# Padding the products of the scans and of the STU to 128 rows, and keeping half of the scan projections in DRAM

**Chip, cores, metric.** One core of a Trainium2 chip (trn2). Time is device microseconds of one execution; lower is better. All runs compared here are of the fast state. "PE" is TensorE, "PEld" its weight loads, DVE VectorE, ACT ScalarE, POOL GpSimd, SP SyncE, which issues nearly all transfers (DMA).

## The reference, cut to what matters

Input is 4 x 48 x 48 x 128 in float32. Layer 0 is a selective scan over the image in four directions (rows, columns, and both backwards); layer 1 is attention and then the STU, a sum of causal convolutions with 16 spectral filters.

```python
# layer 0, of each image; d = 256, N = 16 states, R = 8, K = 4 directions, L = 2304 positions
xs = stack([x0, x1, x0[..., ::-1], x1[..., ::-1]])       # directions 2 and 3 are 0 and 1 backwards
x_dbl = einsum('bkdl,kcd->bkcl', xs, x_proj_w)           # 8 + 16 + 16 rows a direction
dts_r, Bs, Cs = x_dbl[:, :, :R], x_dbl[:, :, R:R+N], x_dbl[:, :, R+N:]
dt = softplus(einsum('bkrl,kdr->bkdl', dts_r, dt_proj_w) + dt_proj_b)
def step(h, inp):
    h = h * exp(dt * A) + (dt * u) * B                   # 256 channels x 16 states
    return h, sum_n(h * C)
# layer 1: t = t + attention(ln(t)); t = t + stu(ln(t))
# stu: for 16 filters k, u convolved with phi_k (and with alternating signs), then projected and summed
```

## The kernel before

The scans run in 24 chunks of 384 positions for each image, a chunk in 8 units (half of the channels, a quarter of the states), a unit as one step ("slot") of a loop that also prepares later chunks and feeds TensorE with pieces of the STU of the image before. Names in the views: xd holds the projections of a chunk, dt, B and y are the products around the scan (`s`), dA its exp, rep holds dt and dt times x for the scans, bc a row of B or C. Of the STU, tt is a piece of the filters, cv a convolution, Q a copy of one by ScalarE, U the sum of both that VectorE makes, pr the projection with the weights G.

```python
class Chunk:
    def prep(self, pool):            # a generator: two steps of it are taken in each slot
        yield
        xd = self.xd = pool.xd.tile([64, CS], F32, ...)                  # two buffers
        bcd = self.bcd = dram.tile([32, CS], F32, ...)
        ps = mm_tile(...)
        for h in range(NH):
            nc.tensor.matmul(ps[:64, :CS], xw[:, h, k, :], in_order(xc[h], k, self.lo, CS), ...)
        yield 2 * CS
        nc.scalar.activation(xd, ps[:64, :CS], AF.Identity, bias=onerow)  # rows: 8 of dt, a one, 32 of B and C
        yield
        for h in range(NH):
            ps = mm_tile(...)
            nc.tensor.matmul(ps[:, :CS], dtw[:, k, h * P:(h + 1) * P], xd[:R + 1], ...)   # 9 rows
            yield CS
            nc.scalar.copy(re[:, h, 0], ps[:, :CS])
            if h == 0:
                nc.sync.dma_start(bcd, xd[32:64])
            yield
        ...                          # softplus, times x, store to DRAM (dtdud)
        load(0)                      # rep: four transfers of 384 KB each, from dtdud
        yield
        yield 0
        load(1)
        yield
    def fetch(self, i, pool):        # a row of B or C, spread over 32 partitions, from bcd
        ...
class Unit:
    def spread(self, ps):            # rows of B to 128 partitions: 32 rows
        nc.tensor.matmul(self.bt[:, :CS], spread[32:64, self.q]..., self.ch.xd[32:64], ...)
    def sum_c(self, ps):             # y: four products side by side, each into 32 partitions
        for g in range(G4):
            nc.tensor.matmul(ch.y[g * DL:(g + 1) * DL, :CS], csum, self.s[:, g], ...)

def prepare(s):                      # twice a slot; ci chunk, j slot in it; TURN = 4
    for c in [ci + 1] * (j <= TURN + 1) + [ci + 2] * (j >= TURN):
        done[0] += next(preps[c], None) or 0

# STU: conv(n, c, g), blocks of 128 rows of u, the last of 64 rows (KP = [128, 128, 128, 128, 64])
x = (sums[:kp, J, g], u[:kp, J, 2 + g], u[:kp, J, g])[c]
nc.tensor.matmul(p2[:, :, at - first:], x, t[:kp, :, ...], ...)
```

## Time and profile before

| | before |
|---|---|
| time, median of the runs | 7045.9 us |
| scan stage 0 (with the mixing of STU weights) | 1090 us |
| scan stages 1, 2, 3 (with the STU of the image before) | 1308, 1307, 1309 us |
| STU of the last image alone, at the end | 743 us |
| attention and the rest | about 1290 us |

A scan stage is counted from the start of its first scan to the start of its last, to about 1 us. The page gives the engines' shares and then forty slices; a digit is tenths of a slice, 9 is 90% or more, and PEclk is the clock that TensorE was granted.

```profile
PE 5958.7 (85%) x25224; PEld 3407.3 (48%) x25224; DVE 4944.7 (70%) x6193; ACT 2846.0 (40%) x5101; POOL 3877.9 (55%) x1815
...
PE   4666666878899999788899999887899999889999
...
PEclk6667676888999999888999999888999999899999
```

The three humps of 9s in the row of PE are scan stages 1 to 3, the last four slices the STU alone. The clock is at 0.8 or more throughout them.

### The profile page before, as it was taken

What the parts mean: (1) busy time and instruction counts of PE and PEld (TensorE: products, weight loads), DVE (VectorE), ACT (ScalarE), POOL (GpSimd) and SP (SyncE); (2) the same over time, 40 slices, a digit from 0 to 9 for tenths busy, and PEclk for the clock granted to TensorE, in tenths of its full rate; (3) what the DMA queues carried; (4) which work ended last, traced back from release to release, by engine and by line L of the source; (5) the groups of instructions that cost most, each with busy time, mean ns of one, the idle gap of its engine ahead of it and who ended that gap; (6) DMA issues with size and microseconds to landing.
All of it is one profiled execution on the core that took longest, in us unless ns stands there. A gap on an engine that the chain in (4) does not pass through costs nothing.

```text
span 7051.1 us, 75955 instructions
## 1 busy us (share of the span) xinstructions
PE 5958.7 (85%) x25224; PEld 3407.3 (48%) x25224; DVE 4944.7 (70%) x6193; ACT 2846.0 (40%) x5101; POOL 3877.9 (55%) x1815
## 2 busy tenths in 40 slices
PE   4666666878899999788899999887899999889999
PEld 1222222533455556533455556533445556547788
DVE  7889898457888987557888987457888987422111
ACT  3555554334444543234445543233444543231000
POOL 2888888126677876115677876205677876300000
PEclk6667676888999999888999999888999999899999
DMA  4655554046777787135777877126777877215545
GB/s 100 138 138 121 139 126 128 19 97 137 165 185 188 193 202 198 42 82 133 165 191 187 202 192 201 48 70 135 164 179 188 204 190 194 76 47 141 157 143 176
DMA packets 648905, 1018.90 MB, mean 145 GB/s; under 512 B 93849, under 2 KB 506649, under 8 KB 623778
## 3 DMA queue, kind: packets, MB, share of 16 engines
q1 hardware_dynamic: 642816, 1010.84, 57.3%
q10 hardware_dynamic: 5698, 3.21, 0.2%
q8 instruction: 201, 3.29, 0.2%
q14 instruction: 190, 1.56, 0.1%
HBM read 895.86 MB, written 117.84 MB: 144 GB/s over the span
## 4 chain that ended last, share of the span: by engine, by line
PE 48%; DVE 24%; DMA 12%; ACT 6%; POOL 4%; issue 4%; SPq 2%; ACTq 0%; DVEq 0%; POOLq 0%
PE cv L926 22%; DVE s L435 12%; PE pr L984 6%; DMA rep<-dtdud 4%; DVE s L427 4%; PE y L452 4%; PE s L687 3%; PE o L680 3%; DMA bc<-bcd 3%; POOL s L444 3%; PE B L419 3%; DVE re L382 2%; DMA tt<-fd 2%; PE xp L350 2%; PE op L623 2%
## 5 line engine op out<-in xcount | busy, mean ns | idle before, releaser
L444 POOL TENSOR_TENSOR s<-s,bc 128x1536 f32<-128x1536 f32 x768 | 2652.0, 3453 | 298.1 <-DVE s L435 195.2
L435 DVE TENSOR_TENSOR_SCAN s<-dA,carry,s 128x384 f32<-128x384 f32 x2560 | 2429.7, 999 | 358.1 <-ACT dA L432 357.6
L432 ACT ACTIVATE dA<-rep,A 128x384 f32<-128x384 f32 x3072 | 1768.5, 584 | 1436.0 <-DVE s L435 1423.5
L926 PE MATMUL cv<-tt,u 128*128 128x256 f32 (+4 forms) x7680 | 1701.8, 362 | 140.3 <-DVE U L946 133.5
L926 PEld LDWEIGHTS cv<-tt,u 128*128 128x128 f32 (+1 forms) x7680 | 1288.1, 193 | 720.9 <-issue 303.7
L946 DVE TENSOR_TENSOR U<-cv,Q 128x256 f32<-128x256 f32 (+1 forms) x1280 | 487.1, 388 | 912.9 <-PE cv L926 910.8
L427 POOL TENSOR_TENSOR s<-rep,bc 128x1536 f32<-128x1536 f32 x288 | 993.2, 3449 | 95.0 <-DMA bc<-bcd 95.0
L926 PE MATMUL cv<-tt,us 128*128 128x256 f32 (+4 forms) x3840 | 897.6, 371 | 149.0 <-DVE U L946 111.2
L452 PE MATMUL y<-s,csum 128*32 128x384 f32 x6144 | 749.3, 563 | 210.9 <-POOL s L444 122.8
L427 DVE TENSOR_TENSOR s<-rep,B 128x1536 f32<-128x1536 f32 x480 | 834.4, 1738 | 94.5 <-PE B L419 57.9
L926 PEld LDWEIGHTS cv<-tt,us 128*128 128x128 f32 (+1 forms) x3840 | 652.3, 197 | 429.7 <-DVE U L946 160.1
L935 ACT COPY Q<-cv 128x256 f32<-128x256 f32 (+3 forms) x640 | 224.7, 352 | 1473.2 <-PE cv L926 1331.3
L984 PE MATMUL pr<-U,G 128*128 128x512 f32 (+4 forms) x2048 | 753.1, 500 | 68.2 <-DVE U L946 36.5
L443 POOL COPY carry<-s 128x4 f32<-128x4 f32 x640 | 145.9, 228 | 1005.4 <-DVE s L435 872.5
L419 PE MATMUL B<-xd,spread 32*128 32x384 f32 x960 | 494.7, 598 | 73.4 <-DVE s L427 72.7
L984 PEld LDWEIGHTS pr<-U,G 128*128 128x128 f32 x2048 | 350.0, 201 | 296.2 <-issue 168.9
L435 DVE TENSOR_TENSOR_SCAN s<-dA,s 128x384 f32<-128x384 f32 x512 | 455.6, 937 | 50.0 <-ACT dA L432 50.0
L452 PEld LDWEIGHTS y<-s,csum 128*32 128x32 f32 x6144 | 128.1, 114 | 658.1 <-issue 318.7
L687 PE MATMUL s<-xnT 128*128 128x512 f32 (+1 forms) x720 | 358.2, 583 | 50.0 <-ACT e L689 26.7
L799 PE MATMUL G<-M,W 128*128 128x128 f32 (+2 forms) x768 | 232.0, 452 | 162.5 <-DMA M<-in_M_phi_plus 109.5
L156 POOL TENSOR_TENSOR ln_vu<-ln_vu,mhalf 128x4 f32<-128x4 f32 (+1 forms) x20 | 31.4, 1572 | 610.6 <-DVE ln_vu L155 610.6
L689 ACT ACTIVATE e<-s,shift 128x512 f32<-128x512 f32 (+1 forms) x360 | 230.8, 644 | 325.7 <-PE s L687 325.4
(155 smaller groups left out, 3965.8 us busy)
## 6 DMA issues: line engine op xcount, KB each, us to landing
rep<-dtdud SPq DMA_DIRECT2D x768, 384.0 KB, 8.4
tt<-fd SPq DMA_DIRECT2D x192, 577.0 KB, 4.6
bc<-bcd SPq DMA_DIRECT2D x2304, 48.0 KB, 3.6
tt<-fd SPq DMA_DIRECT2D x192, 513.0 KB, 4.6
tt<-fd SPq DMA_DIRECT2D x192, 385.0 KB, 4.2
dtdud<-re SPq DMA_DIRECT2D x768, 96.0 KB, 2.2
G<-gd SPq DMA_DIRECT2D x192, 256.0 KB, 4.7
tt<-fd SPq DMA_DIRECT2D x64, 514.0 KB, 5.6
```

Source lines behind the costliest of these rows:

```text
L419: nc.tensor.matmul(self.bt[:, :CS], spread[32:64, self.q].rearrange("p c j -> p (c j)"), self.ch.xd[32:64], start=True, stop=True)
L427: eng.tensor_tensor(s, self.ch.rep[self.h][:, 1], bt.unsqueeze(1).to_broadcast([P, G4, CS]), ALU.mult)
L432: nc.scalar.activation(dA[:, :CS], ch.rep[self.h][:, 0, g], AF.Exp, scale=A[:, ch.k, self.h * G4 + g, self.q:self.q + 1])
L435: nc.vector.tensor_tensor_scan(s, dA[:, CS - 1::-1] if ch.rev else dA[:, :CS], s, 0.0 if ch.first else carry[:, self.h, self.q, g:g + 1], ...
L444: nc.gpsimd.tensor_tensor(self.s, self.s, ch.bc[Q4 + self.q].unsqueeze(1).to_broadcast([P, G4, CS]), ALU.mult)
L452: nc.tensor.matmul(ch.y[g * DL:(g + 1) * DL, :CS], csum, self.s[:, g], start=(self.q == 0), stop=(self.q == Q4 - 1))
L687: nc.tensor.matmul(p[:, :w], xnT[:, i * P:(i + 1) * P], xnT[:, 512 * J:512 * J + w], start=True, stop=True)
L689: nc.scalar.activation(e[:, :w], p[:, :w], AF.Exp, bias=shift)
L799: nc.tensor.matmul(p[:, :n] if j else p[:, NF - 1 - i], W[:, q if t else 0, i], M[t][:, i].unsqueeze(1).to_broadcast([P, n, C]) if j else ...
L926: nc.tensor.matmul(p2[:, :, at - first:], x, t[:kp, :, hi - 1 - at + J * P:end if end >= 0 else None:-1], start=(J == 0), stop=(J == nb - 1))
L946: nc.vector.tensor_tensor(dst, src, q, ALU.add)
L984: nc.tensor.matmul(p[:, :, :v], Gs[n][:, q, x, :], U[n][:, 4 * q:4 * q + 4, :v], start=False, stop=(k == KF - 1 and q == 1 and v == w))
```

## The change

The intent: every product of the scans and of the STU gets 128 rows (zeros in the weights or in the data where there were fewer), so that TensorE does not change its shape between them. And since directions k and k + 2 project the same positions, one product of 128 columns gives both (64 rows each); it is computed for directions 0 and 1, stored to DRAM, and directions 2 and 3 load it. The diff, cut to its core (the layout of the weights on the host follows from it):

```diff
-            xd = self.xd = pool.xd.tile([64, CS], F32, tag="xd", name=f"xd{name}")
-            bcd = self.bcd = dram.tile([32, CS], F32, tag="bcd", name=f"bcd{name}")
-            ps = mm_tile(f"xp{name}")
-            for h in range(NH):
-                nc.tensor.matmul(ps[:64, :CS], xw[:, h, k, :], in_order(xc[h], k, self.lo, CS), ...)
-            yield 2 * CS
-            nc.scalar.activation(xd, ps[:64, :CS], AF.Identity, bias=onerow)
+            xd = self.xd = pool.xd.tile([P, CS], F32, tag="xd", name=f"xd{name}")
+            xdd_ = xdd[k % 2][self.lo // CS]
+            if k < 2:
+                ps = mm_tile(f"xp{name}")
+                for h in range(NH):
+                    nc.tensor.matmul(ps[:, :CS], xw[:, h, k, :], in_order(xc[h], k, self.lo, CS), ...)
+                yield 2 * CS
+                nc.scalar.activation(xd, ps[:, :CS], AF.Identity, bias=onerow)
+            else:
+                yield 0
+                nc.sync.dma_start(xd, xdd_)
             yield
 ...
-                nc.tensor.matmul(ps[:, :CS], dtw[:, k, h * P:(h + 1) * P], xd[:R + 1], ...)
+                nc.tensor.matmul(ps[:, :CS], dtw[:, k, h * P:(h + 1) * P], xd, ...)
                 yield CS
                 nc.scalar.copy(re[:, h, 0], ps[:, :CS])
-                if h == 0:
-                    nc.sync.dma_start(bcd, xd[32:64])
+                if h == 0 and k < 2:
+                    nc.sync.dma_start(xdd_, xd)
 ... # fetch reads its row from xdd; spread has a variant for each half of xd
-            nc.tensor.matmul(self.bt[:, :CS], spread[32:64, self.q]..., self.ch.xd[32:64], ...)
+            nc.tensor.matmul(self.bt[:, :CS], spread[:, self.ch.k // 2, self.q]..., self.ch.xd, ...)
 ... # STU; the unused half of the last block is set to zero once an image
-                x = (sums[:kp, J, g], u[:kp, J, 2 + g], u[:kp, J, g])[c]
-                nc.tensor.matmul(p2[:, :, at - first:], x, t[:kp, :, ...], ...)
+                x = (sums[:, J, g], u[:, J, 2 + g], u[:, J, g])[c]
+                nc.tensor.matmul(p2[:, :, at - first:], x, t[:, :, ...], ...)
```

More of the change, by code (lines that the diff above doesn't have):

```diff
@@ L79, in hybrid_kernel @@
     cb = load("cb", [P, NH], a["conv_b"].rearrange("(h p) -> p h", p=P))
-    xw = load("xw", [P, NH, K, 64], a["x_proj_wT"].rearrange("(h p) k r -> p h k r", p=P))
-    dtw = load("dtw", [R + 1, K, D], a["dt_proj_wT"])
+    xw = load("xw", [P, NH, 2, P], a["x_proj_wT"].rearrange("(h p) k r -> p h k r", p=P))
+    dtw = load("dtw", [P, K, D], a["dt_proj_wT"])
     A = load("A", [P, K, NH * G4, Q4], a["A_logs"])
@@ L114, in hybrid_kernel @@
     nc.vector.tensor_scalar_mul(nident, ident, -1.0)
-    onerow = wp.tile([64, 1], F32, name="onerow")
+    onerow = wp.tile([P, 1], F32, name="onerow")
     nc.vector.memset(onerow, 0.0)
-    nc.gpsimd.affine_select(onerow, onerow, pattern=[[0, 1]], compare_op=ALU.not_equal, fill=1.0,
-                            base=-R, channel_multiplier=1)
-    spread = wp.tile([64, Q4, C4, DL], F32, name="spread")
+    spread = wp.tile([P, 2, Q4, C4, DL], F32, name="spread")
     nc.vector.memset(spread, 0.0)
-    nc.gpsimd.affine_select(spread, spread, pattern=[[-C4, Q4], [-1, C4], [0, DL]],
-                            compare_op=ALU.not_equal, fill=1.0, base=-32, channel_multiplier=1)
+    for v in range(2):
+        nc.gpsimd.affine_select(onerow, onerow, pattern=[[0, 1]], compare_op=ALU.not_equal, fill=1.0,
+                                base=-R - 64 * v, channel_multiplier=1)
+        nc.gpsimd.affine_select(spread[:, v], spread[:, v], pattern=[[-C4, Q4], [-1, C4], [0, DL]],
+                                compare_op=ALU.not_equal, fill=1.0, base=-32 - 64 * v, channel_multiplier=1)
     csum = wp.tile([P, DL], F32, name="csum")
@@ L138, in hybrid_kernel @@
     fd = res.tile([KF, 3, 2, LF + P], F32, name="fd")
+    xdd = [[res.tile([P, CS], F32, name=f"xdd{k}_{c}") for c in range(L // CS)] for k in range(2)]
     def tokens(x, J):
@@ L345, in prep @@
             yield
-            xd = self.xd = pool.xd.tile([64, CS], F32, tag="xd", name=f"xd{name}")
-            bcd = self.bcd = dram.tile([32, CS], F32, tag="bcd", name=f"bcd{name}")
-            ps = mm_tile(f"xp{name}")
-            for h in range(NH):
-                nc.tensor.matmul(ps[:64, :CS], xw[:, h, k, :], in_order(xc[h], k, self.lo, CS),
-                                 start=(h == 0), stop=(h == NH - 1))
-            yield 2 * CS
-            nc.scalar.activation(xd, ps[:64, :CS], AF.Identity, bias=onerow)
+            xd = self.xd = pool.xd.tile([P, CS], F32, tag="xd", name=f"xd{name}")
[3 more added lines that the diff above has]
+                for h in range(NH):
+                    nc.tensor.matmul(ps[:, :CS], xw[:, h, k, :], in_order(xc[h], k, self.lo, CS),
+                                     start=(h == 0), stop=(h == NH - 1))
+                yield 2 * CS
[3 more added lines that the diff above has]
+                nc.sync.dma_start(xd, xdd_)
             yield
@@ L358, in prep @@
                 ps = mm_tile(f"dt{name}_{h}")
-                nc.tensor.matmul(ps[:, :CS], dtw[:, k, h * P:(h + 1) * P], xd[:R + 1], start=True, stop=True)
+                nc.tensor.matmul(ps[:, :CS], dtw[:, k, h * P:(h + 1) * P], xd, start=True, stop=True)
                 yield CS
                 nc.scalar.copy(re[:, h, 0], ps[:, :CS])
-                if h == 0:
-                    nc.sync.dma_start(bcd, xd[32:64])
+                if h == 0 and k < 2:
+                    nc.sync.dma_start(xdd_, xd)
                 yield
@@ L404, in fetch @@
             t = self.bc[i] = pool.one.tile([P, CS], F32, tag=f"bc{i}", name=f"bc{self.name}_{i}")
+            src = xdd[self.k % 2][self.lo // CS]
             for c in range(C4):
-                nc.sync.dma_start(t[c * DL:(c + 1) * DL], self.bcd[4 * i + c].partition_broadcast(DL))
+                row = 64 * (self.k // 2) + 32 + 4 * i + c
+                nc.sync.dma_start(t[c * DL:(c + 1) * DL], src[row].partition_broadcast(DL))
     class Unit:
@@ L418, in spread @@
             self.bt = ps.tile([P, 512], F32, tag="B", name=f"B{self.name}")
-            nc.tensor.matmul(self.bt[:, :CS], spread[32:64, self.q].rearrange("p c j -> p (c j)"),
-                             self.ch.xd[32:64], start=True, stop=True)
+            nc.tensor.matmul(self.bt[:, :CS], spread[:, self.ch.k // 2, self.q].rearrange("p c j -> p (c j)"),
+                             self.ch.xd, start=True, stop=True)
         def enter(self, pool):
@@ L466, in hybrid_kernel @@
     FETCHED = sorted({q for h, q in POOLED} | set(range(Q4, 2 * Q4)))
-    CHUNK_COLS = (len(quads) - len(POOLED)) * CS + len(quads) * CS + 4 * CS
+    CHUNK_COLS = (len(quads) - len(POOLED)) * CS + len(quads) * CS + 3 * CS
     def begin_scans(b, pool):
@@ L810, in begin_stu @@
                  keep.tile([P, NM, 2, C], F32, tag="us", name=f"us{b}"))
+        for t in us[b]:
+            nc.gpsimd.memset(t[KP[-1]:, NM - 1], 0.0)
     def tail(b, J, T, po, pool, ps):
@@ L922, in conv @@
             for J in range(nb):
-                at, kp = max(first, J * P) if J else first, KP[J]
+                at = max(first, J * P) if J else first
                 end = J * P - 1
-                x = (sums[:kp, J, g], u[:kp, J, 2 + g], u[:kp, J, g])[c]
-                nc.tensor.matmul(p2[:, :, at - first:], x, t[:kp, :, hi - 1 - at + J * P:end if end >= 0 else None:-1],
+                x = (sums[:, J, g], u[:, J, 2 + g], u[:, J, g])[c]
+                nc.tensor.matmul(p2[:, :, at - first:], x, t[:, :, hi - 1 - at + J * P:end if end >= 0 else None:-1],
                                  start=(J == 0), stop=(J == nb - 1))
@@ L1125 @@
     l0, l1 = "L0_conv_", "L1_ffn_"
-    xw = np.zeros((D, K, 64), np.float32)
+    xw = np.zeros((D, 2, P), np.float32)
     xp = i[l0 + "x_proj_w"].transpose(2, 0, 1)
-    xw[:, :, :R] = xp[:, :, :R]
-    xw[:, :, 32:] = xp[:, :, R:]
+    dtw = np.zeros((P, K, D), np.float32)
+    for k in range(K):
+        at = 64 * (k // 2)
+        xw[:, k % 2, at:at + R] = xp[:, k, :R]
+        xw[:, k % 2, at + 32:at + 64] = xp[:, k, R:]
+        dtw[at:at + R, k] = i[l0 + "dt_proj_w"][k].T
+        dtw[at + R, k] = i[l0 + "dt_proj_b"][k]
     phi = np.zeros((KF, 2, 2, LF + P + 1), np.float32)
@@ L1139 @@
         "x_proj_wT": xw,
-        "dt_proj_wT": np.concatenate([i[l0 + "dt_proj_w"].transpose(2, 0, 1), i[l0 + "dt_proj_b"][None]]),
+        "dt_proj_wT": dtw,
         "A_logs": i[l0 + "A_logs"].reshape(K, NH * G4, DL, Q4, C4).transpose(4, 2, 0, 1, 3).reshape(P, K, NH * G4, Q4),
```

## The prediction

> **What bounds the kernel now.** I read the page first (engine shares, forty slices), then the table by stage, then the chain of waits, then timelines of single chunks. The scans mark the stages: a prologue, four scan stages (one per batch; 24 chunks of 384 positions, 8 units of four scans each), attention after each, and at the end the spectral filter (STU) of the last batch alone. Scans 1 to 3 run with the STU of the batch before them on TensorE.
>
> ```profile
> core 0: us, PE busy (x) PEld busy (x) DVE busy (x) ACT busy (x) POOL busy (x), PEclk, DMA share, GB/s
> ...
> 124.00:1214.00 1090.00, 681.05 (x2700) 255.28 (x2700) 968.46 (x980) 608.41 (x1090) 934.07 (x423) 0.68 0.56 131
> ...
> 1521.00:2829.00 1308.00, 1185.29 (x5400) 672.03 (x5400) 1088.75 (x1305) 595.76 (x1063) 934.27 (x422) 0.95 0.73 179
> ...
> 6308.00:7051.00 743.00, 734.35 (x3460) 581.45 (x3460) 129.72 (x325) 59.13 (x165) 0.00 (x0) 0.99 0.52 153
> ```
>
> So three regimes. Scan stage 0 is bound by VectorE (89% busy, PE 62%). Scan stages 1 to 3 are bound by PE and VectorE together (91% and 83%); cut at the stage, the chain lies about 47% on PE, 23% on VectorE and 16% on DMA. The end is PE alone (99%). PE time is worth all of itself at the end, about half in stages 1 to 3, almost nothing in stage 0.
>
> The end shows what the change is after:
>
> ```profile
> 6852.47 10.38 PE cv L926 x48
> ...
> 6899.88 8.83 PE cv L926 x60
> 6909.77 8.83 PE cv L926 x60
> ```
>
> Each row is one filter k. The first belongs to columns 384 to 512: 256-column products, 10.38 / 48 = 0.216 us each, the streaming rate. The others belong to the last block, 512 to 576: 128-column products should take half, but 8.83 / 60 = 0.147. Instruction by instruction, 128-row products start 0.112 us apart; a 64-row pair (every fifth block of rows) starts 0.204 after the one before it, its second half 0.215 after its first, the next 128-row product 0.200 after that and its second half again 0.215. Extra: 0.092 + 0.103 + 0.088 + 0.103 = **0.386 us per convolution**. Check: 60 x 0.112 + 4 projections x 0.216 + 6 x 0.386 = 9.89, the period of the rows.
>
> In the scan stages the small products show the same:
>
> ```profile
> 2604.97 0.91 PE L926 MATMUL cv<-tt,u 128*128 128x128 f32 x5
> 2605.81 0.91 PE L419 MATMUL B<-xd,spread 32*128 32x384 f32 x2
> 2606.65 0.85 PE L452 MATMUL y<-s,csum 128*32 128x384 f32 x8
> 2607.43 0.82 PE L926 MATMUL cv<-tt,u 128*128 128x130 f32 x5
> ```
>
> A product is two instructions of 384 x 2 cycles, 0.32 us each. B holds PE 0.84 us (2605.81 to 2606.65) where 0.64 is streaming, and its start comes 0.095 late. The y products (four 32-column strips side by side) are a mode of their own.
>
> **What the Trainium skill says.** "TensorEngine Tiling (Array Packing)", Key Properties: "Changing tiling mode (not just tile) drains the TensorE". The trace agrees: 0.09 to 0.10 us at each change of shape between 128*128 and 64*128, 32*128, 128*64 or 128*32. "TensorE: Matmul & The Clock Gate", LDWEIGHTS: a load's time depends on columns, not rows. The trace agrees, so padding with zeros costs no weight-load time, and the 0.32 us a product streams depends on its columns:
>
> ```profile
> L419 PEld LDWEIGHTS B<-xd,spread 32*128 32x128 f32 x960 | 157.2, 204 | 268.7 <-issue 120.8 <-DVE s L427 110.3 <-DVE s L435 18.9
> ...
> L926 PEld LDWEIGHTS cv<-tt,u 64*128 64x128 f32 x512 | 76.5, 187 | 37.5 <-issue 8.8
> ```
>
> (128-row loads take 193.) "DMA: Bandwidth & Descriptors", Queues, rings and completion order: on each DMA engine descriptors are consumed in ring order. The trace agrees: a small store issued behind big loads on the same queue lands behind them (below).
>
> **The change part by part**, for one of scan stages 1 to 3.
> - Last STU block, 64 rows to 128: 16 filters x 6 convolutions x 0.386 = 37 us of PE, all in the last 4 or so chunks (that block has 17.6% of the STU's columns). The same 37 us at the end of the program.
> - B, 32 to 128 rows: loses the entry (0.095) and the second weight load that nothing hides (0.105); the exit into y's mode stays. 0.20 x 118 = 24 us.
> - dt, 9 to 128 rows, between 128-row products: loses entry, inner reload and exit, 0.29 x 44 = 13 us.
> - x_proj: 1.44 us for an even direction and 2.70 for an odd (strided reading), from start of xp to start of what follows it; mean 2.07, plus 0.095 for entry. Half of them go: 12 x 2.17 = 26 us. The others lose entry and exit, 12 x 0.19 = 2 us.
> - Sum: 102 us of PE per stage, of 1308.
> - Added: for directions 2 and 3, a load of xd (192 KB) from DRAM in place of product and copy. 12 per stage, 2.4 MB against some 234 MB (179 GB/s x 1308 us): bandwidth is no matter. Latency is.
>
> **The new wait.** In program order the load of xd stands directly behind the second rep load of the chunk before, four transfers of 384 KB, and dt follows half a slot later (a slot is a unit's 6.4 us). Chunk 12 of stage 1:
>
> ```profile
> 2138.59 6.76 SPq L376 DMA_DIRECT2D rep<-dtdud  x4
> ...
> 2145.92 0.41 SPq L363 DMA_DIRECT2D bcd<-xd  x1
> ```
>
> ```profile
> 2142.48 0.91 PE L359 MATMUL dt<-xd,dtw 9*128 9x384 f32 x2
> ```
>
> The last rep transfer lands at 2152.4 and the 48 KB bcd store, issued behind it, at 2153.3. A load of xd would land about there, while dt ran at 2142.5. Over chunks 12 to 23 of stages 1 to 3 the rep load lands 6.5 us after the present start of dt (stage means 6.5, 6.7, 6.6), so xd would land some 7.5 us after it. PE works in order: it stands there. ScalarE stands too, at its copy of dt (today 1 us after dt), so exps stop and soon scans. Against it, what ScalarE waits now for x_proj (52.6 us in 21 waits, 2.5 each) goes for half the chunks, and VectorE has a slack of 1 to 2 us. I take 5 to 6.5 us of bubble per such chunk.
>
> Per stage 1 to 3:
> - 12 chunks of directions 0 and 1: PE saves 5 x 0.20 + 2 x 0.29 + 0.19 = 1.8 us each, half of it in time: -11.
> - 8 chunks of directions 2 and 3 before the last block (now 49.3 us each, PE 47.5, VectorE 44): PE saves 1.0 + 0.6 + 2.2 = 3.8, after which VectorE is the floor at about 45 (stage 0 does a chunk in 45.4 with 40.5 of VectorE; this stage's best is 44.9 with 42.8). With the bubble 50 to 51.5: +1 each, +8.
> - 4 chunks under the last block (now 56): PE saves 3.8 + 37 / 4.2 = 12.6; with the bubble 51: -5 each, -20.
> Together -23, times three -69. The end: -37. Stage 0: products hardly count (-10), but where rep loads are late (every third chunk lands 8 us after the copy of dt) the bubble shows, 4 x 6 to 8 us: +15 to +20 net. Setup (a larger dt weight, two memsets): under 3 us. Sum -69 - 37 + 15 = -91, about **6950 us** (-1.4%).
>
> **Rivals.**
> 1. The load is hidden: SyncE runs ahead of PE, or another wait already covers it. Then the 102 us per stage count half to two thirds: 3 x 50 to 65 + 37 = 190 to 230, and stage 0 gains 10: 6810 to 6850. For it: SyncE is often the one waiting (for PE and VectorE). Against it: the rep transfers take 8.4 us from issue to landing, whoever waits.
> 2. The bubble counts in full on top of what VectorE needs, 8 us for 36 chunks, more in stage 0: 36 x 2.5 + 20 more than my sum, near 7060. For it: all engines stop at once, nothing fills the gap.
> 3. VectorE takes over at once and PE time is worth nothing in the scans: only the 37 us of the end are left, less the bubbles: 7010 or above. Against it: chunks under the last block have PE 95% and VectorE 79% busy.
>
> **Range and chances.** The 37 us at the end are nearly certain. The rest is a difference of two effects of the same size, both about 50 to 80 us per stage; a bubble 1.5 us shorter than mine moves the total by 60 us and over the 2% line (6905). Hence 6950, range 6850 to 7060; faster 0.25, within 2% 0.72, slower 0.03.
>
> **What would show each step right or wrong.** Right: the end stage at 706 us, with 60 products in about 6.7 us; no shapes 9*128, 32*128, 64*128 left in scans and STU, B to y 0.74 us; xp x192. PE waits for the DMA xd<-xdd some 36 to 48 times, 5 to 8 us each, in the view of waits, and ScalarE's wait for dt grows by as much; chunks of directions 2 and 3 are no shorter than those of 0 and 1 late in the stage. Wrong: waits for xdd under 2 us (rival 1), an end stage that stays at 740 (then drains are not from the shape), or stages 1 to 3 over 1310 us (rival 2).

## The result, and the profile after

The changed kernel is correct and takes 7256.9 us (median of 4, 7254.6 to 7261.3): a ratio of 1.029 (95% interval 1.028 to 1.031), slower by 2.9%, where 6950 was predicted with a range of 6850 to 7060. A ratio here is the mean time of one kernel's fast runs over that of the other's of the same rounds, so not quite the ratio of the medians.

| us | before | after | difference |
|---|---|---|---|
| scan stage 0 | 1090 | 1126 | +36 |
| scan stage 1 | 1308 | 1380 | +72 |
| scan stage 2 | 1307 | 1371 | +64 |
| scan stage 3 | 1309 | 1384 | +75 |
| STU at the end | 743 | 707 | -36 |

The attention between them changed by under 2 us each time; the five rows give the difference. First what went as intended. In the chain of waits of the kernel after, the last block at the end stands so:

```profile
7110.31 10.38 PE cv L937 x48
...
7142.57 6.70 PE cv L937 x60
```

60 products in 6.70 us, not 8.83: 0.112 each, as the drains' removal should give, while the 256-column block before it keeps its 10.38. The shapes 9*128, 32*128 and 64*128 are gone from the scans and the STU, and TensorE's busy time fell from 5959 to 5642 us. Yet the kernel is slower. The table by stage, with stage 1 cut in three (the chunks before any load of xd is made, the stretch of twelve chunks in which all twelve are made, the rest), before, then after:

```profile
1521.00:2108.00 587.00, 510.37 (x2021) 263.06 (x2022) 470.88 (x570) 257.37 (x462) 388.17 (x181) 0.91 0.69 161
2108.00:2719.00 611.00, 572.97 (x2743) 337.59 (x2741) 531.38 (x626) 298.97 (x525) 473.07 (x214) 0.98 0.78 198
2719.00:2829.00 110.00, 101.95 (x638) 71.38 (x638) 86.49 (x111) 39.42 (x79) 73.03 (x29) 0.95 0.59 166
```

```profile
1557.00:2125.00 568.00, 479.54 (x2006) 268.49 (x2008) 459.37 (x568) 255.39 (x460) 389.13 (x181) 0.92 0.71 168
2125.00:2833.00 708.00, 558.10 (x2723) 361.52 (x2722) 530.64 (x627) 293.88 (x515) 470.73 (x213) 0.89 0.68 174
2833.00:2938.00 105.00, 86.47 (x628) 65.87 (x628) 84.48 (x111) 39.65 (x78) 73.81 (x30) 0.93 0.61 172
```

Columns: from and to, length, then busy time of PE, PEld, DVE, ACT and POOL, granted clock, DMA share, GB/s. The first part gains 19 us, the last 5; the middle loses 97. There all engines do the same work as before (DVE 531 us in both) in more time, and the clock falls from 0.98 to 0.89. The view of waits of the kernel after (who waited for whom: us in total, times, longest) and of the load's line say why:

```profile
ACT re L368 <- PE dt L366: 480.1, 127, 14.0
...
PE dt L366 <- DMA xd<-xdd: 359.6, 42, 12.5
```

```profile
DMA to landing us min/median/max: 7.3/8.5/11.5
```

TensorE stops 42 times at dt, 8.6 us on average, for a transfer that takes 8.5 us (median) from issue to landing. ScalarE's wait for dt was 166.4 us before. One stop in the timeline (start, length, engine, what, and in brackets what the engine waited for):

```profile
2388.05 2.00 PE L937 MATMUL cv<-tt,u 128*128 128x258 f32 x8 [0.46 <-DVE U L957]
...
2398.72 1.65 PE L366 MATMUL dt<-xd,dtw 128*128 128x384 f32 x2 [8.67 <-DMA tt<-fd]
...
2400.16 3.62 PE L937 MATMUL cv<-tt,us 128*128 128x256 f32 x8
...
2400.41 0.48 ACT L368 COPY re<-dt 128x384 f32<-128x384 f32 x1 [9.63 <-PE dt L366]
2403.82 0.37 ACT L946 COPY Q<-cv 128x256 f32<-128x256 f32 x1 [2.94 <-PE cv L937]
2404.09 1.09 ACT L441 ACTIVATE dA<-rep,A 128x384 f32<-128x384 f32 x2
...
2404.72 1.93 DVE L444 TENSOR_TENSOR_SCAN s<-dA,carry,s 128x384 f32<-128x384 f32 x2 [11.90 <-ACT dA L441]
```

The load was issued at 2389.89 behind four rep transfers (2386.52 to 2389.47). PE stands 8.67 us (the weight load of the same product names xd<-xdd). ScalarE, in order, stands at its copy of dt, then at a copy that needs a convolution behind dt, and only then comes the exp; VectorE stands 11.90. This way through ScalarE is not the usual one: read from the trace, VectorE's longest wait around the stop ends in 24 of the 36 stops of stages 1 to 3 at U, which needs a convolution that stands behind dt on TensorE itself, and in 12 at a scan that needs ScalarE's exp. And the 8 convolution instructions after the stop take 3.62 us where 8 of the same size took 2.00 before it: they run at half clock. The Trainium skill, "TensorE: Matmul & The Clock Gate", Part 1, says that after an idle window of some 3.4 us the clock falls to a half. The trace agrees: TensorE is idle from 2390.06, the clock record stands at 0.5 from 2394.10 to 2404.34, and 1.0 and 0.5 are its only values.

### The profile page after: what moved, and what is told of

It reads as the page before. It is cut to its first block, busy times and chain, and to the rows that moved or that the text cites. A ratio compares the mean times of both kernels' runs of the same rounds, so it can differ in the third digit from the quotient of the medians.

```text
span 7259.6 us, 75560 instructions
## 1 busy us (share of the span) xinstructions
PE 5641.7 (78%) x25032; PEld 3440.7 (47%) x25032; DVE 4893.1 (67%) x6193; ACT 2822.0 (39%) x5053; POOL 3881.9 (53%) x1825
## 4 chain that ended last, share of the span: by engine, by line
PE 40%; DVE 26%; DMA 19%; ACT 5%; issue 4%; SPq 3%; POOL 2%; DVEq 0%; ACTq 0%; POOLq 0%
PE cv L937 18%; DVE s L444 14%; DMA xd<-xdd 5%; PE pr L995 5%; DVE s L436 4%; DMA tt<-fd 4%; DMA bc<-xdd 4%; PE s L696 3%; DMA rep<-dtdud 3%; PE y L461 3%; PE o L689 3%; DVE re L389 2%; PE op L632 2%; PE B L428 2%; DVE xc L264 2%
## 5 line engine op out<-in xcount | busy, mean ns | idle before, releaser
L937 PE MATMUL cv<-tt,u 128*128 128x256 f32 (+3 forms) x7680 | 1680.3, 366 | 285.1 <-DVE U L957 279.6
L937 PEld LDWEIGHTS cv<-tt,u 128*128 128x128 f32 x7680 | 1305.9, 199 | 827.3 <-DVE U L957 360.7
L937 PE MATMUL cv<-tt,us 128*128 128x256 f32 (+3 forms) x3840 | 841.3, 362 | 111.3 <-DVE U L957 61.5
L461 PE MATMUL y<-s,csum 128*32 128x384 f32 x6144 | 730.6, 551 | 199.2 <-POOL s L453 122.3
L937 PEld LDWEIGHTS cv<-tt,us 128*128 128x128 f32 x3840 | 645.7, 198 | 309.1 <-DVE U L957 107.4
L995 PE MATMUL pr<-U,G 128*128 128x512 f32 (+4 forms) x2048 | 731.6, 491 | 65.5 <-DMA G<-gd 43.5
L428 PE MATMUL B<-xd,spread 128*128 128x384 f32 x960 | 444.9, 548 | 111.2 <-DVE s L436 110.9
L366 PE MATMUL dt<-xd,dtw 128*128 128x384 f32 x384 | 212.6, 643 | 398.1 <-DMA xd<-xdd 359.6
```

The source lines that it names most:

```text
L428: nc.tensor.matmul(self.bt[:, :CS], spread[:, self.ch.k // 2, self.q].rearrange("p c j -> p (c j)"), self.ch.xd, start=True, stop=True)
L937: nc.tensor.matmul(p2[:, :, at - first:], x, t[:, :, hi - 1 - at + J * P:end if end >= 0 else None:-1], start=(J == 0), stop=(J == nb - 1))
L995: nc.tensor.matmul(p[:, :, :v], Gs[n][:, q, x, :], U[n][:, 4 * q:4 * q + 4, :v], start=False, stop=(k == KF - 1 and q == 1 and v == w))
```

## The experiments

Theory A: the wait for xd, caused by the load's place behind rep, is the whole loss, and padding gains. Rivals: B, padding or the new spread of the work slows the scans; C, the traffic of the load costs wherever it stands.

| run | edit | us, median | ratio to before (95%) | stages 0 / 1 / 2 / 3 | end |
|---|---|---|---|---|---|
| after | the change | 7256.9 | 1.029 (1.028-1.031) | 1126 / 1380 / 1371 / 1384 | 707 |
| e1_early | load 5 slots earlier | 6869.2 | 0.973 (0.971-0.975) | 1072 / 1265 / 1261 / 1271 | 707 |
| e2_nold | no load: products for all directions | 6887.1 | 0.975 (0.973-0.977) | 1082 / 1265 / 1259 / 1270 | 707 |
| e3_ldonly | before plus the load (wrong result) | 7481.8 | 1.061 (1.057-1.064) | 1129 / 1438 / 1438 / 1438 | 743 |
| e6_warm | after, 8 idle products at the stop | 7248.8 | 1.026 (1.024-1.029) | 1147 / 1364 / 1373 / 1374 | 707 |
| e8_warm13 | after, 13 idle products | 7243.4 | 1.028 (1.025-1.030) | 1157 / 1364 / 1354 / 1361 | 707 |
| e7_early64 | e1_early, last block 64 rows again | 6927.6 | 0.982 (0.980-0.985) | 1072 / 1274 / 1267 / 1279 | 743 |
| e5_first | after, load ahead of rep | 6921.7 | 0.982 (0.980-0.984) | 1078 / 1282 / 1281 / 1278 | 707 |
| e4_actq | after, load on ScalarE's queue | 6961.8 | 0.988 (0.986-0.990) | 1092 / 1289 / 1291 / 1288 | 707 |
| e9_copylater | after, ScalarE's copy a slot later | 7420.9 | 1.053 (1.050-1.055) | 1156 / 1421 / 1420 / 1423 | 707 |
| e10_early_copylater | e1_early, copy a slot later | 6993.3 | 0.992 (0.990-0.995) | 1093 / 1306 / 1296 / 1304 | 707 |

Before took 7063.2, 7052.1 and 7052.7 us (medians) on the chips of the three groups of runs (e1, e2, e3, e6; e7, e8, e5, e4; e9, e10), so medians of different groups compare to some 17 us only. All but e3_ldonly are correct.

**The load, earlier.**

```diff
+        def load_xd(self, pool):
+            self.xd = pool.xd.tile([P, CS], F32, tag="xd", name=f"xd{self.name}")
+            nc.sync.dma_start(self.xd, xdd[self.k % 2][self.lo // CS])
 ... # in prepare, first call of a slot
+            if first_half and j == 0 and ci + 2 < len(chunks) and chunks[ci + 2].k >= 2:
+                chunks[ci + 2].load_xd(front)
 ... # in prep, directions 2 and 3: no load; pool xd=(2, SB) -> xd=(3, SB)
```

> The changed kernel, but the load of xd for directions 2 and 3 is issued about five slots (some 30 us) earlier, at slot 0 of the chunk two before, ahead of both rep loads, into a third xd buffer; same bytes, same products. Theory A (the wait: the load stands behind 1.5 MB of rep in the same queue, and TensorE, ScalarE and VectorE stop for it, 7 us of VectorE 12 times in stage 0 and 9.5 to 10.4 us 36 times in stages 1 to 3): the stops vanish and the gain of padding and of the dropped products is left: 6800 to 6880 us, waits for xd<-xdd under 20 us in all. Rival B (the padded products or the new spread of filter work over the slots slow the scans): stays above 7100. Rival C (the extra DRAM traffic itself, wherever it stands): above 7200.

Measured 6869 us, as theory A has it; the fastest of all. The load's line, and stage 1 in the same three parts as above:

```profile
DMA to landing us min/median/max: 2.3/2.6/4.7
```

```profile
1503.00:2071.00 568.00, 483.32 (x2006) 270.90 (x2010) 458.75 (x568) 255.74 (x460) 389.59 (x181) 0.91 0.71 168
2071.00:2661.00 590.00, 525.03 (x2722) 343.51 (x2714) 530.93 (x627) 294.86 (x515) 470.56 (x213) 0.96 0.82 209
2661.00:2768.00 107.00, 87.33 (x628) 66.95 (x628) 84.83 (x111) 39.99 (x78) 74.43 (x30) 0.92 0.61 169
```

With the same bytes and products, only the middle differs from the changed kernel by more than 2 us, 590 us against 708. Rivals B and C fall. (This run has a third xd buffer too; e5_first below has two and most of the gain.) Twelve stops in a stage cost 1380 - 1265 = 115, 109 and 113 us: **9.4 us each**; in stage 0, 54 us, 4.5 each.

**Padding alone.**

```diff
-            if k < 2:
+            if True:
-                    nc.tensor.matmul(ps[:, :CS], xw[:, h, k, :], ...
+                    nc.tensor.matmul(ps[:, :CS], xw[:, h, k % 2, :], ...
```

> Padding alone: all products with 128 rows, but x_proj is computed for all four directions as before (96 products, each 128 columns wide), no load of xd. Theory A: before minus 37 us at the end minus some 40 per stage of scans 1 to 3 (75 us of TensorE less in each, half of it in time): 6850 to 6930. Rival B (padding slows the scans): 7050 or more.

Measured 6887 us, as expected. It is 18 us (of medians) from e1_early. So half of the x_proj products, some 26 us of TensorE a stage, is worth next to nothing: stages 1 to 3 are the same to 3 us, stage 0 differs by 11. That is a sum: in chunks 12 to 19 the early load is 9 us a stage shorter than this run, under the last block (chunks 20 to 23) 8 longer (mean of stages 1 to 3, read from the traces). The load had little to win.

**The load alone.**

```diff
+            if k < 2:
                 ... # as before
+            else:
+                yield 0
+                nc.sync.dma_start(xd, xdd_)          # 64 rows; 9, 32 and 64-row products stay
```

> The load alone, in the kernel before: products unpadded as before, but directions 2 and 3 load xd (64 rows) from DRAM at the place where the change loads it, in place of x_proj. The result is wrong on purpose (they get the projections of directions 0 and 1). Theory A: the changed kernel plus what padding gains, 7350 to 7450. Rival B: 7040 to 7100, the load costs little and padding is what slows.

Measured 7482 us, 32 above the expected range: the stops cost at least as much in the kernel before (+130 us in each of stages 1 to 3, +39 in stage 0).

**Is it the clock?** The same product, of weights without meaning, over and over into the PSUM tile that dt then overwrites.

```diff
                 ps = mm_tile(f"dt{name}_{h}")
+                if h == 0 and k >= 2:
+                    for i in range(8):               # 13 in e8_warm13
+                        nc.tensor.matmul(ps[:, :CS], win[:, :P], win[:, :CS], start=True, stop=True)
```

> The changed kernel with 8 products of no use (384 columns, two instructions each, 5.1 us at full clock) ahead of the first dt of each chunk of directions 2 and 3, where TensorE stands for 8.4 us anyway. It tests whether a part of the loss is the clock: in the changed kernel the second half of stage 1 has 22 spells at half clock, with 93 us of products in them, against 5 and 22 before. If the half clock after each stop costs about 35 us per stage: 7140 to 7200 us, and the spells fall back to under 10. If the stop alone is the cost: 7250 to 7310, unchanged or a little slower.

> As the run with 8 products of no use, but 13 (8.4 us, the mean length of the stop), because after 8 there were still stops of about 4 us and the products after them still ran at half clock. If half clock after the stop is worth some 35 us a stage: 7130 to 7200 and the second half of stage 1 has under 30 us of products at half clock (93 in the changed kernel, 62 with 8). If the stop alone is the cost: 7240 to 7300 although the half clock is gone.

8 products left stops of about 4 us behind them, and the products after those still ran at half clock (17 spells, not under 10); the total, 7249, is 1 us under the range for the stop alone: no test. 13 close the gap. Second half of stage 1, by the table: the changed kernel, then e8_warm13.

```profile
2244.00:2938.00 694.00, 552.29 (x2940) 369.60 (x2940) 524.58 (x631) 284.63 (x507) 467.52 (x212) 0.90 0.67 176
```

```profile
2250.00:2950.00 700.00, 634.65 (x3283) 416.87 (x3285) 537.53 (x646) 294.40 (x520) 476.65 (x214) 0.96 0.69 179
```

The clock is back at 0.96 (0.98 in the kernel before), products at half clock (matmuls laid over the clock records) fall from 93 to 47 us, though not under the 30 that I had set; e1_early, which has no stops, stands at 44. Half of the 46 us is 23, about what the stages gain: stages 1 to 3 gain 17, 17 and 23 us; stage 0, where the idle products outlast the stop, loses 31, and the total, 7243, lies in the range that I gave for the stop alone. So half clock is a part, about 1.6 us of the 9.4 per stop (19 / 12), and the stop itself is the rest. As the 13 products outlast the shorter stops, 1.6 is rather too low.

**Where does the gain under the last block go?** In e1_early, stages 1 to 3 gain 43, 46 and 38 us over before; my sum had -87 ahead of its bubbles (a chunk at VectorE's floor of 45 plus a bubble of 5.3 makes the 50.3 behind its "+1 each"; twelve such bubbles are 64, and -23 less 64 is -87).

```diff
-                at = max(first, J * P) if J else first
+                at, kp = max(first, J * P) if J else first, KP[J]
 ... # and [:kp] again on both operands
```

> The version with the early load, with the padding of the filter's last block undone (64-row products there again, 96 per batch). It asks where the 37 us of TensorE go that the padding saves in the last quarter of each scan stage 1 to 3. At the end of the program it costs 37 us in any case. Theory A1 (under the last block the scan stages are bound by transfers: with the early load the chunks 20 and 21 take 58 and 61 us, no less than the 57 and 57 of the kernel before, TensorE waits 21 us for tt there and the DMA moves 213 GB/s): the scan stages stay within 8 us each and the total is the early load's plus 37 to 60, 6905 to 6930. Rival A2 (TensorE bounds there, something else made those chunks long): plus 37 and 20 or more in each of three stages, 6965 or above.

Measured: the end +36 us, but stages 1 to 3 only +9, +6 and +8, though 37 us of TensorE by my sum come back in each (its busy time in stage 1 rises by 30, from 1095.7 to 1125.5): A1, at the edge of its limit (total 6928). By the table, the first three chunks under the last block before (2605 to 2779) and with the early load (2541 to 2725):

```profile
2605.00:2779.00 174.00, 164.59 (x992) 111.73 (x990) 135.65 (x170) 69.95 (x132) 116.61 (x58) 0.97 0.80 220
```

```profile
2541.00:2725.00 184.00, 147.62 (x999) 112.38 (x1000) 135.79 (x171) 70.89 (x132) 118.23 (x58) 0.90 0.80 213
```

and who waits there with the early load:

```profile
PE cv L944 <- DMA tt<-fd: 21.3, 6, 5.6
```

The windows hold the same three chunks of scans, not exactly the same pieces of the STU, but their message is plain: 17 us less of TensorE, no shorter, at 213 and 220 GB/s. Before, PE waited 0.7 us for tt in its stretch, and was busy for 95% of it. Over all four chunks (mean of stages 1 to 3, read from the traces) TensorE is busy 33 us less and idle 27 us more, mainly 16 for tt and 11 for VectorE at U. So transfers take most of what padding gains there, and VectorE the rest; no run changes the transfers alone, so how much they would give back is not shown.

**The load's place in the queue.**

```diff
-            for c in [ci + 1] * (j <= TURN + 1) + [ci + 2] * (j >= TURN):     # e5_first
+            for c in [ci + 2] * (j >= TURN) + [ci + 1] * (j <= TURN + 1):
 ...
-                nc.sync.dma_start(xd, xdd_)                                   # e4_actq
+                nc.scalar.dma_start(xd, xdd_)
```

> The changed kernel with one thing turned round: in the half slot where both are issued, the load of xd comes before the four rep transfers, not behind them. Same products, bytes and buffers. Theory A (its place behind 1.5 MB in the same queue makes the wait): the load lands 2 to 4 us after issue, not 8.8, most stops go: 6870 to 6960. Rival C (a load from DRAM just before use is too late wherever it stands in that half slot): 7100 or above.

> The changed kernel with the load of xd issued from ScalarE's queue and not from SyncE's, at the same point of the program. If the place in SyncE's queue is what counts, the load overtakes: landing 2 to 5 us after issue, 6880 to 7000. If it is the shared engines, busy with rep, that count: landing 7 us or more, 7150 or above.

Both are within their ranges, 6922 and 6962 us. With e5_first TensorE waits for xd 79.6 us in all (34 times), not 359.6. The landing takes 7.3 us in the median and not the 2 to 4 that I expected, because the first of the two rep loads still stands ahead: when the load of xd is issued, one to three of its four transfers are under way, against all four of the second in the changed kernel and none in e1_early. In all three runs each of the 48 loads lands after everything that SyncE issued before it. (The edit turns round all steps of the two chunks in these slots, not the load alone.) With e4_actq the median landing is short:

```profile
DMA to landing us min/median/max: 2.2/2.8/8.2
```

TensorE waits 20.7 us in all. But against what I expected the load does not overtake: for 22 of 48 loads no rep transfer was under way, and 14 that met three or four of them took 4.1 to 8.2 us; none landed ahead of a rep transfer. ScalarE mostly just issues it before SyncE issues the second rep load, so the range was met without what it was meant to show. This fits the Trainium skill, "Trainium Kernel Development and Optimization", Key Constraints, by which issuing DMAs from several engines concurrently "only saves the sequencer's issue time". The run is 93 us above e1_early, about 20 in stage 0 and 17 to 30 in the others. SyncE's own waits show what is new in it:

```profile
SPq L383 <- DMA xd<-xdd: 273.3, 30, 11.7
SPq L415 <- DMA xd<-xdd: 126.5, 15, 11.5
SPq L910 <- DMA xd<-xdd: 38.8, 3, 14.6
```

Once for each load, 439 us in all, a later transfer of SyncE's waits until the load from ScalarE's queue has landed (0.2 us in all in e1_early), and TensorE's waits for tt rise to 131 us from 74. That these waits make up the 93 us is likely, but no run tests it.

**Which engine carries the stop to VectorE?**

```diff
                 yield CS
+                if h == 0:
+                    yield
+                    yield 0
                 nc.scalar.copy(re[:, h, 0], ps[:, :CS])
 ... # two idle steps after store(1) taken out
```

> The changed kernel with the load where the change has it, but ScalarE's copy of the first dt product one slot later in program order (two idle steps of the preparation are taken out further on, so that its end stays where it was). TensorE still stands at dt for the load; ScalarE should go on with the exps of one more slot. It asks which engine carries the stop to VectorE, where I had taken 5 to 6.5 us per stop and it costs 9.4 in stages 1 to 3. If it is ScalarE, in order behind its copy: TensorE's wait for xd stays near 8 us, VectorE's stop shrinks by 4 us or more, and the total is 7060 to 7160. If TensorE's own stop reaches VectorE just as fast (through B, U and the full PSUM buffers): 7220 to 7280.

> Control for the run before: the version with the early load and the same later copy. If the later copy in itself gains or costs nothing, 6855 to 6885 as with the early load alone; whatever it differs from that is taken off the reading of the run before. It is also the last candidate for the fastest version.

My guess was ScalarE, and it failed: 7421 is outside both ranges, and so is the control. The control shows that the later copy costs 124 us by itself (6993 against 6869), so only the difference of the pair counts: 7421 - 6993 = 428 us with the copy later, 7257 - 6869 = 388 with it in its place (401 by the ratios to before, as these two are of different groups). VectorE's longest stop around TensorE's does not shrink (11.8 us for 9.6, mean of stage 1), and it ends at U, for a convolution behind dt, in 9 of 12 stops (8 in the changed kernel). VectorE's waits for convolutions (DVE U, on PE) rise from 1083 to 1172 us in all, and TensorE's for xd from 360 to 458. So TensorE's stop reaches VectorE without ScalarE's copy, through the convolutions: the second case of the expectation in kind, with a total that the later copy itself put out of its range. This pair also tells how much the spacing of those steps is worth, which I did not look into.

## Why the prediction was wrong, point by point

- **The drains: right.** End stage 707 for 706, 60 products in 6.70 us for "about 6.7", B to y 0.74 us. TensorE's busy time in stage 1 falls by 90 us in e1_early (1185.3 to 1095.7), for the 102 of the sum.
- **The wait: right in kind, place and count, and just over the range in length.** "PE waits for the DMA xd<-xdd some 36 to 48 times, 5 to 8 us each": 42 times, 8.6 us; the wait of ScalarE for dt grew by 314 us beside the 360 of TensorE.
- **Failed step 1, the size of the bubble:** "I take 5 to 6.5 us of bubble per such chunk", from "VectorE has a slack of 1 to 2 us" and ScalarE's lost waits for x_proj, and from a path by which "exps stop and soon scans". A stop costs 9.4 us in stages 1 to 3 (early load against change). The slack did not show: VectorE's longest stop around dt is 9.6 us on average in stage 1, longer than TensorE's 8.4; in 24 of 36 stops it stands at U for TensorE's convolutions, a path that the prediction lacks; and half clock, which I had not thought of, adds about 1.6. In the sum the stops stood as 12 x 5.3 = 64 us a stage (the difference between -87 and -23); they are 113. That is 147 us for three stages.
- **Failed step 2, the gain under the last block:** "4 chunks under the last block (now 56) ... -5 each", that is 41 us a stage before the bubble, from TensorE's saving down to VectorE's floor of 45 us a chunk. The 37 us of TensorE are worth 6 to 9 us a stage (e7_early64): TensorE then waits for tt and for VectorE instead. Chunk by chunk (first scan to the next chunk's first, mean of stages 1 to 3), chunks 20 to 23 take 58.4 us before (the 56 is that of stage 1) and 56.9 with the early load; chunks 12 to 19 49.2 and 46.8, for the floor of 45; chunks 0 to 11 56.8 and 55.4. In all, the change without stops gains 42 us a stage and not 87; of the 45 missing, 35 are under the last block and 15 in chunks 12 to 19, while the first twelve gain 6 more than I wrote. That is 134 us for three stages.
- **Failed step 3, stage 0:** 15 to 20 us for "every third chunk". All twelve loads stopped VectorE there (1.4 to 11.0 us, 7.0 on average in the trace), at a cost of 54 us, against a gain of 18: +36, for +15.
- Together 147 + 134 + 21 us, and the end 1 us short: the 302 or so between -91 and +211. Rival 2, the bubble in full with nothing to fill the gap, named the direction; its 7060 still rested on the gain of step 2.
- The range was too narrow for what I had written: a difference of two effects of the same size, both only estimated, each wrong by half in the same direction.

## What to carry to other kernels

A transfer that takes the place of a product must be issued as early as its landing time behind everything already in its queue, not half a step ahead of its use: the same load of 192 KB cost 388 us behind 1.5 MB and nothing that could be seen five slots earlier. In stages 1 to 3 a stop of the engine that feeds all others was paid in full, with the clock on top (9.4 us for stops of 8.7 on average); in stage 0, where VectorE bounds, it cost 4.5. Slack of the other engines should not be subtracted unless the trace shows it in that stretch. And what a faster engine gains in a stretch is capped by the next limit there: look at the waits and the DMA rate of that stretch, not of the stage.

## What the Trainium skill lacked or had wrong

- "TensorEngine Tiling (Array Packing)", Key Properties, says that a change of mode drains TensorE but gives no size: here 0.09 to 0.10 us at each change, and another 0.10 for the second weight load after it; together 0.386 us more for each convolution with one 64-row block between 128-row ones.
